# Gathers by step, resident down weights and another order of work in an attention and mixture-of-experts layer

## The chip, the cores and the metric

The kernel runs on one core of a Trainium2 chip. Its metric is the time of one execution on the device, in microseconds (us). A core has a matrix engine (TensorE, PE in the profile, with its weight loads as PEld), a vector engine (VectorE, DVE), a scalar engine (ScalarE, ACT), a general engine (GpSimd, POOL) that here also issues the indirect DMAs, and a sync engine (SyncE, SP) that issues nearly all other DMAs. Each engine works through its own queue of instructions in order. The engines wait for one another by semaphores.

## The reference

One transformer layer on four batches of 512 tokens with 256 features: attention with 16 heads and a linear position bias, a layer norm, a mixture of 64 experts of which each token takes 8, a shared expert, and a second layer norm.

```python
x = _layernorm(x + attention(x))              # 16 heads of 16, causal, ALiBi
logits = x @ gate_w.T                         # 2048 tokens x 64 experts
topv, topi = jax.lax.top_k(logits, 8)
rw = softmax(topv)                            # the weights of a token's 8 experts
W = zeros((N, E)).at[arange(N)[:, None], topi].set(rw)
gate, up = split(einsum('nh,eih->nei', x, gu_w))
inter_w = silu(gate) * up * W[:, :, None]
out = einsum('nei,ehi->nh', inter_w, dp_w)    # the down projection of each expert
out = out + sigmoid(x @ sh_gate1_w.T) * shared_expert(x)
x = _layernorm(x + out)
```

## The kernel before, in words

**Steps.** The experts are worked through in 16 steps of four experts (`QUAD`) for each of the four batches: 64 steps in all. This text calls them by batch and step, 0.0 to 3.15. A 128-token tile (there are four, t = 0 to 3, in a batch) has 30 places for an expert (`CELL`; 32 in the last four steps of batch 3), so that a step has 120 rows of tokens for each expert.

Four strands make a step. `gather` (letter g, L1020) brings the tokens to their places with matmuls against one-hot tiles (`px`), which ACT and DVE copy to `xt`; a pass serves four steps. `up` (u) first issues the load of the step's down weights `dq` on SP (L1038, 256 KB), then 32 matmuls `gu` (L1049), a tanh on ACT (L1057) and two products on DVE (L1058, L1059). `down` (d) multiplies with `dq` (L1081), copies the result `yq` with ACT (L1093) and writes it to DRAM, `rows_out`, from SP (L1094).

**The way back.** A token takes its eight results from `rows_out` by eight indirect gathers. `route` computes, for each token, the rows of its eight experts sorted from the largest (place k = 0) to the smallest (k = 7); as a step's rows are contiguous, a higher row is a later step. `fetch` (i) issues one gather per tile and place on POOL (L1160), 128 in all, into a ring of 8 buffers `got`; the slice of `rows_out` that the instruction names decides which writes it must wait for. `combine` (c) multiplies each gathered tile by its weight and adds it to `x` on DVE (L1171), and after a tile's last place comes the layer norm (L607 to L626) and the store. Gather n into the ring waits until combine n - 8 has read its buffer.

**The late steps.** The last four steps of batch 3 (3.12 to 3.15, `LATE`) aren't gathered: their results stay on chip (L1088, in the place of used weights), weights spread over the rows come from DRAM (`spread_in`, w, four DMAs on SP each), DVE masks them (`weigh`, e, L1120), and `collect` (k) multiplies and adds them (L1135, L1143). So the gathers of batch 3 need steps 3.0 to 3.11 alone. For batches 0 to 2, places 4 to 7 need steps up to 14 and places 0 to 3 all 16. In batch 3 every gather of before names the whole buffer, all twelve steps.

**What sets the order.** Nothing is left to a scheduler. Each strand is a Python generator; a string `ORDER` of one letter per turn (p projection, s scores, v context, o output, r routing, and those above) says which strand goes on next. So an instruction's place in its engine's queue is written out by hand, and each engine meets the strands in that order. A closing check (z) of three products `fine` and `fits` sets a flag; if it is set, a second, general program computes everything again.

**Memory.** `cxT` (two buffers), `scale` (two) and `avs` (two) belong to the attention and are idle once it is over. `dq` has four buffers.

Of the kernel before, what the change touches and what calls it, by code (L numbers as in the profile page):

```python
# [8 lines left out]
FP = mybir.dt.float32  # L9
# [3 lines left out]
ALU = mybir.AluOpType  # L13
AX = mybir.AxisListType

P = 128
HEADS, HD = 16, 16
# [9 lines left out]
ROOM = 32  # L27
GROUP = 16
# [9 lines left out]
    "pppppspppspsppsvvvsppvsvsvsvsvvspsovsvpsvvvspsppopposvvsvsoovsrrrvvsvspsvvvrhrosrrsvvsvrhrsvsrsrprhh"  # L38
    "rgvvvspogspprvphphporshvrvvsoorsprrgsvvvgsroghsvrgsrvvrvsrrsvsgvvsorvsrrgvvorsvsrosorsorrrrvvsvsvvvv"
    "tuguugguuggrhglogrgdrruuugrddrruuurrdorlgguuruuggdgrougrudgogrugllrugdudduggruuggrghrhhuuhgdhhdguuuu"  # L40
    "ghddgrrhugudguudrghgriiirgdgiguggruuuiiiuugicigcduigucigdcrgdigcuucgciuugddrczcccgigciiiiricduruuigg"
    "igugrgcguuiggcdgcihhucudhcuuhicddiughuuudcihggiiciugucddgirchhuiguuugdgcgccddggicciciuuucugcgguccgud"
    "guigciiicduccddccgcguugccggguiiguicchccuudugiiidcciigiiiiguucugigdgccuuigigchcidhiucduhhiuducghdchuu"
    "cgguudchcigghcuudigcuiugdgcidccdcigicuuiggcicuiguigiuccgudugggiiucicidcdccdcccruuccgggguuiciigcuwwug"
    "gccdugidgiiicichdgiuccugccggieguccugecuiiiicdiiduuuiucciccdcduiddwciicciiicicicuuiuuucciwccicciccccc"
    "uceecckdiiidkciicdciickicicicckicicckicicicicciiiiiiicickickiiccccccccccckcccz"
# [363 lines left out]
def kernel(  # L410
# [329 lines left out]
    def context():  # L740

        for b in range(B):
            cxT = cxs[b] = mpool.tile([P, KC, S], FP, tag="cxT", name=f"cxT_{b}", bufs=2)
            for c, par, n in units:
# [15 lines left out]
                avs = mpool.tile([P, S], FP, tag="avs", name=f"avs_{b}_{c}_{par}", bufs=2)  # L760
# [17 lines left out]
    def output():  # L778

        for b in range(B):  # L780
            scales = []
            for c in range(KC):
# [5 lines left out]
                scale = mpool.tile([P, S], FP, tag="scale", name=f"scale_{b}_{c}", bufs=2)  # L788
                for h in range(HEADS // KC):
                    nc.sync.dma_start(  # L790
                        out=scale[HD * h : HD * (h + 1), :],
                        in_=turned[b][part][h : h + 1, :].to_broadcast([HD, S]),
                    )
                scales.append(scale)
# [5 lines left out]
            for c in range(KC):  # L800
                nc.vector.tensor_tensor(cxT[:, c, :], cxT[:, c, :], scales[c], ALU.mult)
# [13 lines left out]
    codes, ats, w8s, shares = {}, {}, {}, {}  # L815

    def route():

        for b in range(B):
# [48 lines left out]
            nc.vector.tensor_tensor(row, row, chosen, ALU.mult)  # L868
            r8 = small.tile([P, NT, TOP], FP, tag="r8", name=f"r8_{b}")
# [6 lines left out]
            if not LATE[b]:  # L876
                part = slice(TOP // 2, TOP)
                nc.vector.tensor_scalar(at[:, :, part], near[:, :, part], SOON[b] - QUAD * SLOTS - 1.0, None, ALU.min)
# [28 lines left out]
            if LATE[b]:  # L907
# [6 lines left out]
                nc.vector.memset(rest[:, :, FIRST[b] :], 0.0)  # L914
# [9 lines left out]
                for t in range(NT):  # L924
                    nc.tensor.transpose(pt[: 2 * EL, t * P : (t + 1) * P], pair[:, t].rearrange("p w e -> p (w e)"), ident)
                flip = rpool.tile([P, TOP, NE], FP, tag="pick", name=f"flip_{b}", bufs=2)
# [106 lines left out]

    def up():

        for n, (b, q) in enumerate(steps):
            dq = late["pool"].tile([P, QUAD // 2, E], FP, tag="dq", name=f"dq_{b}_{q}", bufs=4)
            nc.sync.dma_start(out=dq, in_=dp[:, 2 * q : 2 * q + 2, :])  # L1038
# [86 lines left out]
    def collect():  # L1125

        for b in range(B):
# [13 lines left out]
            for t in range(NT):  # L1141
                part = xs[b][:, t, :]
                nc.vector.tensor_tensor(part, acc[t // 2][:, t % 2, 0:E], part, ALU.add)  # L1143
                yield
# [4 lines left out]
    for b in range(B):  # L1149
        if LATE[b]:  # L1150
            moves += [(b, t, k) for t in range(NT) for k in range(TOP)]
        else:
# [134 lines left out]
```

## Time and profile before

| | us |
|---|---|
| median of three runs | 483.08 (480.72 to 483.99) |
| the profiled execution | 479.91 |
| its span, first to last instruction | 477.4 |
| PE busy | 423.1 (89%) |
| DVE busy | 339.7 (71%) |
| ACT busy | 244.8 (51%) |
| POOL busy | 205.6 (43%) |

The profile is of one execution. A group's line gives: source line, engine, operation, result<-operands, shapes, count, then busy time and mean duration in ns, then the idle time of that engine just before, with what ended it. A row of the timeline starts with the start and the length in us; a bracket at its end is the idle time before it and its releaser. "DMA a<-b" in the chain is the wait for that transfer. The 40 slices of the page are 11.9 us each and hold tenths of busy time; PEclk is the clock that TensorE was granted.

### The profile page before, as it was taken

Reading aid. Unit: us, or ns where it says so; the run is one execution under the profiler, and the core shown is the slowest. Engines: PE = TensorE matmul, PEld = TensorE weight load, DVE = VectorE, ACT = ScalarE, POOL = GpSimd, SP = SyncE. Lnnn points to the kernel's source line nnn. Section 1 sums busy time; section 2 is a strip of 40 time slices with the busy share of each in tenths; the row PEclk is TensorE's granted clock in tenths of the full one; section 3 lists DMA queues with packets and bytes.
Section 4 is the critical chain, followed back from the end, with each engine's and each line's share of the span. In section 5 each row is a group of like instructions: output and inputs, shape, how many; then the busy total and the mean of one; then the engine's idle time right before and its main releaser. Section 6 shows DMA issues by size and latency. Waiting matters only on the chain.

```text
span 477.4 us, 12454 instructions
## 1 busy us (share of the span) xinstructions
PE 423.1 (89%) x4887; PEld 284.3 (60%) x4887; DVE 339.7 (71%) x922; ACT 244.8 (51%) x454; POOL 205.6 (43%) x238
## 2 busy tenths in 40 slices
PE   8999999998999989999999999999999997878100
PEld 3535454453644556876878778777787775765100
DVE  1522326798976888986786798889778898487474
ACT  2658647773578734446646547563566545322000
POOL 6424522253324610310027664266553666457771
PEclk9999999999999999999999999999999999897855
DMA  7900110000000043886868969889899899798342
GB/s 215 405 36 5 28 25 3 24 7 24 3 25 28 8 170 99 260 284 250 240 161 280 284 210 299 267 241 305 267 283 317 255 289 325 231 278 212 105 105 74
DMA packets 37238, 82.68 MB, mean 173 GB/s; under 512 B 8276, under 2 KB 14548, under 8 KB 36148
## 3 DMA queue, kind: packets, MB, share of 16 engines
q1 hardware_dynamic: 30484, 64.51, 43.1%
q0 software_dynamic: 6144, 16.79, 12.1%
q8 instruction: 40, 0.66, 0.6%
q10 hardware_dynamic: 544, 0.52, 0.3%
q14 instruction: 26, 0.21, 0.1%
HBM read 49.88 MB, written 31.92 MB: 171 GB/s over the span
## 4 chain that ended last, share of the span: by engine, by line
PE 68%; DVE 12%; DMA 8%; ACT 4%; issue 3%; POOL 2%; SPq 1%; DVEq 0%; POOLq 0%; ACTq 0%
PE gu L1049 19%; PE y L1081 11%; PE px L1020 9%; PE sT L724 8%; PE av L752 6%; DMA got<-rows_out,at 4%; PE pv L695 3%; PE pq L678 3%; PE pk L678 3%; PE po L808 2%; DMA dq<-in_dp_dram 2%; ACT yq L1093 2%; PE plT L828 2%; DVE x L1171 1%; PE sh L889 1%
## 5 line engine op out<-in xcount | busy, mean ns | idle before, releaser
L1160 POOL DMA_INDIRECT got<-rows_out,at x128 | 125.5, 980 | 128.8 <-DVE x L1171 57.8
L1049 PE MATMUL gu<-xt,gu_sb 128*64 128x120 f32 (+1 forms) x2048 | 118.9, 271 | 1.4 <-DVE ma L1059 1.4
L1049 PEld LDWEIGHTS gu<-xt,gu_sb 128*64 128x64 f32 x2048 | 106.2, 138 | 16.8 <-issue 14.1
L729 ACT ACTIVATE pr<-sT 128x768 f32<-128x768 f32 (+1 forms) x96 | 79.5, 884 | 29.4 <-PE sT L724 29.2
L734 POOL TENSOR_SCALAR_AFFINE_SELECT pr<-pr 128x512 f32<-128x512 f32 x64 | 41.8, 666 | 83.5 <-ACT pr L729 80.7
L1081 PE MATMUL y<-dq,ma 64*120 64x256 f32 (+1 forms) x512 | 68.5, 393 | 8.9 <-DMA dq<-in_dp_dram 5.6
L1093 ACT COPY yq<-y 120x1024 f32<-120x1024 f32 x60 | 59.9, 1012 | 29.4 <-PE y L1081 24.6
L1171 DVE SCALAR_TENSOR_TENSOR x<-got,w,x 128x256 f32<-128x256 f32 x128 | 62.7, 493 | 15.2 <-DMA got<-rows_out,at 13.5
L1081 PEld LDWEIGHTS y<-dq,ma 64*120 64x120 f32 (+1 forms) x512 | 44.5, 182 | 21.4 <-DVE x L1171 4.1
L1057 ACT ACTIVATE ma<-gu 128x240 f32<-128x240 f32 (+1 forms) x64 | 23.7, 371 | 59.9 <-PE gu L1049 51.5
L1010 ACT COPY xt<-px 128x192 f32<-128x192 f32 (+1 forms) x128 | 44.7, 365 | 17.0 <-PE px L1020 13.3
L724 PE MATMUL sT<-qT,kT 32*128 32x256 f32 (+3 forms) x512 | 51.9, 468 | 0.0
L1010 DVE COPY xt<-px 128x480 f32<-128x480 f32 x64 | 41.4, 650 | 14.2 <-ACT xt L1010 13.9
L942 POOL TENSOR_TENSOR pick<-pick,rest 128x512 f32<-128x512 f32 x16 | 21.3, 1334 | 48.2 <-ACT rest L903 25.3
L1020 PE MATMUL px<-hot,xh 64*128 64x288 bf16 x256 | 37.5, 287 | 4.8 <-ACT xt L1010 3.7
L752 PE MATMUL av<-pr,va 128*32 128x128 f32 (+3 forms) x512 | 40.2, 438 | 0.8 <-POOL pr L734 0.8
L1058 DVE SCALAR_TENSOR_TENSOR ma<-ma,gu 128x240 f32<-128x240 f32 (+1 forms) x64 | 25.6, 400 | 18.6 <-ACT ma L1057 18.4
L1020 PE MATMUL px<-hot,xl 64*128 64x288 bf16 x256 | 37.0, 283 | 0.0
L1020 PE MATMUL px<-hot,xm 64*128 64x288 bf16 x256 | 37.0, 282 | 0.0
L724 PEld LDWEIGHTS sT<-qT,kT 32*128 32x128 f32 x512 | 24.4, 183 | 19.7 <-issue 11.5
L752 PEld LDWEIGHTS av<-pr,va 128*32 128x32 f32 x512 | 13.8, 109 | 28.4 <-issue 17.6
L1059 DVE TENSOR_TENSOR ma<-gu,ma 128x240 f32<-128x240 f32 (+1 forms) x64 | 26.1, 408 | 2.2
(148 smaller groups left out, 488.6 us busy)
## 6 DMA issues: line engine op xcount, KB each, us to landing
rows_out<-yq SPq DMA_DIRECT2D x60, 480.0 KB, 5.2
dq<-in_dp_dram SPq DMA_DIRECT2D x64, 256.0 KB, 5.3
gu_sb<-in_gu_dram SPq DMA_DIRECT2D x8, 1024.0 KB, 11.1
scale<-turned SPq DMA_DIRECT2D x64, 32.0 KB, 1.8
got<-rows_out,at POOLq DMA_INDIRECT x128
gu_sb<-spread SPq DMA_DIRECT2D x16, 128.0 KB, 7.3
x<-in_x_dram SPq DMA_DIRECT2D x3, 512.0 KB
out_dram<-x SPq DMA_DIRECT2D x6, 256.0 KB
```

The costliest lines, as they stand in the source:

```text
L678: nc.tensor.matmul(ps, w_sb[n][:, kc, c * P : (c + 1) * P], xT[:, kc, :], start=(kc == 0), stop=(kc == KC - 1),)
L724: nc.tensor.matmul(s_ps[r // 2][:, r % 2, lo : lo + widths[m]], kTs[b][rows, c, kb * P : (kb + 1) * P], qTs[b][rows, c, par, kb * P :], st ...
L729: nc.scalar.activation(pr[:, 2 * i : 2 * i + 2, :], s_ps[i][:, :, : sum(widths)], AF.Exp, scale=1.0 / HD**0.5)
L734: nc.gpsimd.affine_select(out=pr[:, :, lo : lo + P], in_=pr[:, :, lo : lo + P], pattern=[[0, 4], [1, P]], compare_op=ALU.is_ge, fill=0.0, ...
L752: nc.tensor.matmul(av[32 * r : 32 * r + 32, kb * P :], vas[b % 2][:, kb, 8 * c + 2 * r + par, :], pr[:, r, lo : lo + w], start=(kb == 0), ...
L1010: copy(xt[:, kc, :, t * wide + lo : t * wide + hi], ps[:, kc, lo * GROUP : hi * GROUP].rearrange("p (s e) -> p e s", e=GROUP),)
L1020: nc.tensor.matmul(ps[:, kc, first : first + WIDTH * GROUP], parts[b][i][PART * half : PART * half + PART, t, kc * P : (kc + 1) * P], o[PA ...
L1049: nc.tensor.matmul(gu_ps[64 * e : 64 * e + 64, j, which, :], gu_sb[p // GUC][:, p % GUC, kc, which, 64 * e : 64 * e + 64], xt[:, kc, QUAD ...
L1081: nc.tensor.matmul(ys[:, e, j, :], a[64 * e : 64 * e + 64, j, :], dq[64 * e : 64 * e + 64, j, :], start=True, stop=True,)
L1093: nc.scalar.copy(yq.rearrange("s j e h -> s e j h"), ys)
L1160: nc.gpsimd.indirect_dma_start(out=g, out_offset=None, in_=rows_out[b][0 : SOON[b] - (QUAD * SLOTS if not LATE[b] and k >= HALF else 0)], ...
L1171: nc.vector.scalar_tensor_tensor(acc[:, t, :], got.pop(n), w8s[b][:, t, k : k + 1], acc[:, t, :], ALU.mult, ALU.add)
```

## The change

1. `BEFORE`: a gather for place k = 4, 5, 6, 7 names only the rows of the steps up to 1, 2, 3, 4 before the last (`reach`). This holds for batch 3 as well, counted from its twelve early steps. Routing clamps the row numbers place by place and multiplies a test of each into `fits`. The late steps' rows are cleared ahead of the sort in batch 3, so that its eight places count early rows alone.
2. Gathers and combines go by place: all four tiles of place 7, of 6, 5 and 4, then tile by tile places 0 to 3.
3. The down weights of steps 8 to 15 are loaded once, in batch 0, into buffers of the attention (two of `cxT`, one of `scale`, one of `avs`), and stay. 24 of 64 `dq` loads go. For this `scale` and `avs` become one buffer of two halves each.
4. `collect` adds two tiles at once (two instructions where there were four).
5. `ORDER` is another string.

```diff
+BEFORE = (0, 0, 0, 0, 1, 2, 3, 4)
...
+                if par == 0:
+                    both = mpool.tile([P, KC, S], FP, tag="avs", name=f"avs_{b}_{c}")
+                avs = both[:, par, :]
...
+    def reach(b, k):
+        return SOON[b] - BEFORE[k] * QUAD * SLOTS
...
+            if LATE[b]:
+                nc.vector.memset(row[:, :, FIRST[b] :], 0.0)
...
-            if not LATE[b]:
-                part = slice(TOP // 2, TOP)
-                nc.vector.tensor_scalar(at[:, :, part], near[:, :, part], SOON[b] - QUAD * SLOTS - 1.0, None, ALU.min)
+            for k in range(TOP):
+                if BEFORE[k]:
+                    end = reach(b, k) - 1.0
+                    nc.vector.tensor_scalar(at[:, :, k], near[:, :, k], end, None, ALU.min)
+                if BEFORE[k] > 1:
+                    nc.vector.scalar_tensor_tensor(
+                        fits[:, 0:NT], near[:, :, k], end + 0.5, fits[:, 0:NT], ALU.is_le, ALU.mult
+                    )
...
+    def stay(n):
+        bed, place = divmod(n, 2)
+        if bed not in beds:
+            tag, bufs = (("cxT", 2), ("cxT", 2), ("scale", 1), ("avs", 1))[bed]
+            old = mpool.tile([P, KC, S], FP, tag=tag, name=f"bed{bed}", bufs=bufs)
+            beds[bed] = old.rearrange("p k s -> p (k s)").rearrange("p (i w e) -> p i w e", i=2, w=QUAD // 2)
+        return beds[bed][:, place]
...
-            dq = late["pool"].tile([P, QUAD // 2, E], FP, tag="dq", name=f"dq_{b}_{q}", bufs=4)
-            nc.sync.dma_start(out=dq, in_=dp[:, 2 * q : 2 * q + 2, :])
+            if q < NQ // 2:
+                dq = late["pool"].tile([P, QUAD // 2, E], FP, tag="dq", name=f"dq_{b}_{q}", bufs=4)
+            elif b == 0:
+                stays[q] = dq = stay(q - NQ // 2)
+            else:
+                dq = stays[q]
+            if q < NQ // 2 or b == 0:
+                nc.sync.dma_start(out=dq, in_=dp[:, 2 * q : 2 * q + 2, :])
...
     for b in range(B):
-        if LATE[b]:
-            moves += [(b, t, k) for t in range(NT) for k in range(TOP)]
-        else:
-            moves += [(b, t, k) for t in range(NT) for k in range(HALF, TOP)]
-            moves += [(b, t, k) for t in range(NT) for k in range(HALF)]
+        moves += [(b, t, k) for k in range(TOP - 1, HALF - 1, -1) for t in range(NT)]
+        moves += [(b, t, k) for t in range(NT) for k in range(HALF)]
...
-                out=g, out_offset=None, in_=rows_out[b][0 : SOON[b] - (QUAD * SLOTS if not LATE[b] and k >= HALF else 0)],
+                out=g, out_offset=None, in_=rows_out[b][0 : reach(b, k)],
```

The last two lines of the two order strings show the fifth point; i and c are gathers and combines, u, d and k the matmuls of up, down and collect:

```
before: "gccdugidgiiicichdgiuccugccggieguccugecuiiiicdiiduuuiucciccdcduiddwciicciiicicicuuiuuucciwccicciccccc"
        "uceecckdiiidkciicdciickicicicckicicckicicicicciiiiiiicickickiiccccccccccckcccz"
after:  "dgicucgcuwuiigcchgcuucuuiigccgduuiiggcdgddcicicgiiiuucccccicgcugidwuiicgccudigiccccgcdciiuuueicicucc"
        "ucidiiuwwuuiiiiudciciecudidekccidikckiciciezcicickicicickicicickicccckccccccccccz"
```

## The prediction

> **What bounds the kernel now.** I read the page first, then the chain that ended last, then the timeline of PE and POOL in the last 80 us, then busy time by stage.
>
> ```profile
> span 477.4 us, 12454 instructions
> PE 423.1 (89%) x4887; PEld 284.3 (60%) x4887; DVE 339.7 (71%) x922; ACT 244.8 (51%) x454; POOL 205.6 (43%) x238
> ...
> PE   8999999998999989999999999999999997878100
> ...
> POOL 6424522253324610310027664266553666457771
> PEclk9999999999999999999999999999999999897855
> ```
>
> PE is full for 33 slices and gone in the last three. So there are two parts: a long one that PE sets, and a tail that something else sets. What is it? The timeline of POOL and DVE from 426 us on:
>
> ```profile
> 426.54 0.94 POOL L1160 DMA_INDIRECT got<-rows_out,at  x1 [3.48 <-DMA gu_sb<-spread]
> 427.79 1.07 POOL L1160 DMA_INDIRECT got<-rows_out,at  x1 [0.30 <-DVE x L1171]
> ...
> 465.98 1.07 POOL L1160 DMA_INDIRECT got<-rows_out,at  x1 [0.30 <-DVE x L1171]
> ...
> 469.05 0.48 DVE L1171 SCALAR_TENSOR_TENSOR x<-got,w,x 128x256 f32<-128x256 f32 x1 [0.27 <-DMA got<-rows_out,at]
> ...
> 472.44 0.41 DVE L626 TENSOR_SCALAR x<-x,mv,rstd 128x256 f32<-128x256 f32 x1
> ```
>
> From 426.54 to 467.05 POOL issues 32 gathers back to back, one in 40.51/32 = 1.27 us: all of batch 3. Nothing else waits for long there; this is the tail. From the last gather's end to the span's end are 10.35 us: landing, a combine, a late add, the last norm and the store. The first gather waited for rows: the named releaser is the transfer beside them, but the instruction names the whole buffer, and the last rows in it are those of step 3.11. That step's down matmul is here, in PE's timeline:
>
> ```profile
> 402.71 1.03 PE L1081 MATMUL y<-dq,ma 64*120 64x256 f32 x8
> 407.42 1.61 PE L1081 MATMUL y<-dq,ma 64*120 64x256 f32 x8 [3.67 <-DMA dq<-in_dp_dram]
> 408.95 4.64 PE L1049 MATMUL gu<-xt,gu_sb 128*64 128x120 f32 x64
> ...
> 417.34 1.13 PE L1081 MATMUL y<-dq,ma 64*120 64x256 f32 x8
> ```
>
> 3.11 starts at 417.34; its rows can be gathered 9.2 us later (copy, write, landing), and the end comes 60.1 us after it. The reader also sees the one large PE stall: 3.8 waits 3.67 us for its `dq`, and runs slowly afterwards, 1.61 against 1.03, and 4.64 for two ups against 3.50 at 182.65 us. By stage (PE, PEld, DVE, ACT, POOL busy, clock, DMA share, GB/s):
>
> ```profile
> 360.00:400.00 40.00, 38.26 (x548) 29.76 (x544) 34.02 (x97) 22.05 (x45) 21.00 (x22) 1.00 0.93 279
> 400.00:417.30 17.30, 13.62 (x176) 11.25 (x172) 10.76 (x25) 6.15 (x10) 8.84 (x10) 0.90 0.85 289
> sum 248.60, PE 237.31 PEld 185.67 DVE 201.57 ACT 132.72 POOL 100.96; mean PE 33.90 PEld 26.52 DVE 28.80 ACT 18.96 POOL 14.42
> ```
>
> The sum is over 168.7 to 417.3 us, where the experts are worked through: PE 95%, DVE 81%. Before 400 us PE is idle for 11.97 us in all, then 3.67.
>
> **The change part by part.** The same PE work stands ahead of 3.11 in both listings of the instructions, and the same behind it (three ups, four downs, the four groups of collect). So I ask when 3.11 starts, and how long the end is behind it.
>
> *Down weights.* 24 loads of 256 KB leave SP and the DMA engines, 6.3 of 82.7 MB. Worth on the path: the stall of 3.67 and the slow stretch after it, (1.61 - 1.03) + (4.64 - 3.50) = 1.72. 3.11 would start at 417.34 - 5.39 = 411.95. The other loads were hidden behind PE work; steps 0 to 7 stay as they were, 5 to 7 us of PE work ahead of their use, against 5.3 us to landing. New is that the load of 0.10 takes the buffer of `cxT` right after the last matmul that reads it and stands 5.7 us of PE work ahead of its use: between 0 and the 3.67 of the stall above, I take +1, as it is nearest to the loads that just fit. The halves of `avs` and `scale` fall free a unit later, ten us of attention: 0, bound by the 1.5 us of PE's largest stall there.
>
> *The tail.* Place 7 now needs rows up to 3.7, 6 up to 3.8, 5 up to 3.9, 4 up to 3.10, and 16 gathers of places 0 to 3 need 3.11. If POOL were free, 16 x 1.27 = 20.3 us would follow the rows: last gather 9.2 + 20.3 = 29.5 us after 3.11 starts. But POOL is not free. PE work from 3.8 to 3.11 is about 9.5 us (ups 1.86, downs 1.03, gather halves 0.4), so 3.8's rows come about when 3.11 starts, and 28 gathers then take 35.5 us, with a little waiting between: last gather 29.5 to 33 us after 3.11. Behind it, norms now overlap: the twelfth of the 16 ends 5.1 us before the last, lands in 2.5, add 0.7, norm of three tiles 4.57 (459.69 to 464.26), four combines 2.0, last norm 2.86, store 4.55: 12.1 us behind the last gather. The end is thus 41.6 to 45 us behind the start of 3.11; I take 44, for 60.1 before: -16. PE's own rest takes 26 us now (417.34 to 443.57) and is done by then.
>
> *DVE.* This is the bill. The new order puts 18 more combines (0.49 each), two more norms (4.0 each, 429.21 to 433.24) and the new clamps ahead of 3.11: per batch four at 0.27 and three at 0.16, less one of 0.30 in three batches, 5.3 us. 8.9 + 8.0 + 5.3 = 22 us, less a masking of 0.75, to the 201.57 in 243 us: 92%. If they fit into DVE's gaps they cost nothing, as combines did up to now; if the gaps are all needed, 21 us. Where it is tight is the stretch from 2.15 to 3.11: counted by letter, DVE goes from some 41 to 51 us there (41 combines, 2.5 norms, 13 ups at 0.81, 12 copies at 0.65), against 46.5 us of PE. So at least 4.5; I take 6.
>
> *Combines that wait.* DVE is in order: a combine that waits for rows holds the products behind it, which PE's downs need. From a step's down to its gather took 9.2 us from its start at 3.11, and a gather's data takes 2 to 3 more, some 12 us. Before, the first combine stood 12.8 us of PE work or more behind the step it needs, outside the tail. Now 8.1 us for place 7 of batch 0, 10.8 for 6 and 7 of batch 2, and 9.4, 6.8 and 5.5 in batch 3 (where DVE's lag, counted above, covers the wait). 0 to 4 us each; I take +2.5, for the first.
>
> POOL's 0.3 us between gathers and `collect` (two adds of 0.7 for four of 0.42) stay where they are. Sum: 411.95 + 1 + 6 + 2.5 = 421.5 for 3.11, + 44 = 465.5 for the span, + 2.51 (479.91 - 477.4) = **468**. The profiled execution is 0.7% under the median of the runs; the change is -12, 2.5%.
>
> A rule of the Trainium skill speaks against the change. The gathers' mean is 980 ns, with 940 the least and 1345 the most, beside a DVE that is 85% busy from 360 to 400 us.
>
> ```profile
> L1160 POOL DMA_INDIRECT got<-rows_out,at x128 | 125.5, 980 | 128.8 <-DVE x L1171 57.8
> ...
> L1171 DVE SCALAR_TENSOR_TENSOR x<-got,w,x 128x256 f32<-128x256 f32 x128 | 62.7, 493 | 15.2 <-DMA got<-rows_out,at 13.5
> ```
>
> By "SBUF — State Buffer", section "Who interferes with whom", DVE and GpSimd hold a shared pair of ports exclusively, and the one that comes second waits for the whole instruction. By that, gathers beside a fuller DVE would stretch; the trace shows it at 4% over the least, so it is a rival only.
>
> **The rivals.**
> *PE alone* (15%). DVE fits into its gaps, no combine waits: 3.11 at 412, + 41.6 to 44, + 2.5 = 456 to 458.5. For it: DVE is idle for 47 us in this stretch now. Against: the last 50 us are full.
> *DVE takes the bound* (13%). All 21 us become path, 3.11 at 434, + 44 + 2.5 = 480.5: no change. For it: 92% on an engine that both waits for PE and is waited for.
> *Combines block the queue* (11%), the slower side. If the early combines hold DVE and through it PE, with rows and gathers as late as behind 3.11 in the trace (gather at 426.54, its combine at 433.44: 16 us from the down), the shortfalls are 8 (batch 0), 5 (batch 2) and 6.6, then some 3 each for the next two in batch 3, which stack: 25 us, and DVE's 6: 3.11 at 443, end 490. It decides from about 4 us over the 12 that I take.
> *Ports* (3%). Each of the 28 gathers at 1345 instead of 980: +10, 478.
> *No finer waits, or the guard* (3%). If a gather still waited for all rows, the tail keeps 60: 484. But the listing shows a different DMA semaphore for places 6, 5, 4 and 0. The second program would cost hundreds of us; worked through for these inputs, no token's row passes a bound.
>
> **How the numbers follow.** Forecast 55% (461 to 475), rivals 15, 13, 11, 3, 3. The likeliest gives 468. Leaving out the slow end of the rivals and half of the fast one's, 454 to 482 holds 8 in 10. One per cent, about what a measurement here tells from no change, is 478.2 to 487.9. Faster: 55 + 15 + 3 + a part of the DVE case, 0.76; the same: the rest of that case and the unchanged tail, 0.13; slower 0.11.
>
> **What would show it.** Right: no `dq` wait behind batch 0; 3.11's down near 421; POOL gathering without a gap from about then, 21 or so gathers behind it instead of 32; the end 42 to 45 us behind 3.11; DVE over 88% in the expert stage. Wrong: PE waiting for `ma` products by more than 10 us in all, DVE waiting for `got` by more than 10 us ahead of 3.11, or POOL idle for rows in the tail.

## The result, and the profile after

The changed kernel takes 477.73 us (median; 474.31 to 483.01), the kernel before on the same chip 481.62: a ratio of 0.9906 (0.9881 to 0.9931). Run once more beside other kernels it gave 0.9948 (0.9908 to 0.9987). So the gain is 0.5 to 0.9%, under the one per cent that the prediction gives as what a measurement tells from no change; 2.5% was forecast. The profiled execution took 478.21 us, with a span of 476.5, 0.9 less than before. The page of the changed kernel, parts 1 and 2:

```profile
span 476.5 us, 12378 instructions
PE 427.4 (90%) x4887; PEld 287.3 (60%) x4887; DVE 337.5 (71%) x946; ACT 244.2 (51%) x454; POOL 204.5 (43%) x238
...
PE   8999999989999999999989999899899989976900
...
POOL 6433522255513610220145556255661677364770
PEclk9999999999999999999989999999999999898965
```

PE is now at work one slice longer, with a hole (7 and 6) just ahead, and POOL's row, full in the last slices before, has holes too (the 3 and the 4 near its end). PE's timeline where step 3.5, step 3.6 with 3.7, and step 3.11 go down:

```profile
405.76 1.13 PE L1115 MATMUL y<-dq,ma 64*120 64x256 f32 x8 [1.80 <-DMA dq<-in_dp_dram]
407.33 3.67 PE L1115 MATMUL y<-dq,ma 64*120 64x256 f32 x16
...
431.78 2.07 PE L1115 MATMUL y<-bed,ma 64*120 64x256 f32 x8 [3.66 <-DVE marks L1151]
```

3.8's wait for weights is gone, as forecast; 3.5 waits instead, and 3.11 for its products (`marks` is only the instruction right behind them). And 3.11 starts at 431.78, where 421.5 was forecast and 417.34 was measured before. The end comes 44.7 us behind it (forecast 44, before 60.1). These rows of POOL's timeline are the starts that stand behind a gap of over 0.5 us, and the last gather:

```profile
409.60 0.94 POOL L1191 DMA_INDIRECT got<-rows_out,at  x1 [0.87 <-DVE x L1202]
...
416.97 0.94 POOL L1191 DMA_INDIRECT got<-rows_out,at  x1 [6.43 <-DVE x L1202]
...
423.58 0.94 POOL L1191 DMA_INDIRECT got<-rows_out,at  x1 [1.84 <-DVE rstd L625]
...
433.65 0.94 POOL L1191 DMA_INDIRECT got<-rows_out,at  x1 [5.37 <-DVE x L1202]
...
463.29 0.95 POOL L1191 DMA_INDIRECT got<-rows_out,at  x1 [0.30 <-DVE st L609]
```

416.97 is batch 3's first gather (place 7), 433.65 the first of place 5, which needs the rows of 3.9. Before, all 32 gathers ran without a gap; now they lose 6.9 us: from first start to last 46.3 us, where 31 spacings of 1.27 are 39.4. The gaps at 416.97, 423.58 and 433.65 are not the ring's, as the combines that free these buffers had ended by 415.50, 417.46 and 425.35; they are waits for the rows of 3.7, 3.8 and 3.9.

What holds up 3.5's weights and 3.9's rows stands in SP's queue (start, length with issue time, number):

```profile
394.53 3.59 SPq L1141 DMA_DIRECT2D gu_sb<-spread  x4
398.16 2.18 SPq L1072 DMA_DIRECT2D dq<-in_dp_dram  x3
...
417.91 0.32 SPq L1128 DMA_DIRECT2D rows_out<-yq  x1
418.32 3.03 SPq L1141 DMA_DIRECT2D gu_sb<-spread  x4
421.57 1.08 SPq L1128 DMA_DIRECT2D rows_out<-yq  x1
```

The new order puts the loads of the late steps' spread weights (w, four of 128 KB a step) ahead of the loads for 3.5 to 3.7, and between the rows of 3.8 and 3.9. In the kernel before, the first eight of them stood together, ahead of the weights of 3.7 and of the steps behind it:

```profile
387.12 7.07 SPq L1107 DMA_DIRECT2D gu_sb<-spread  x8
394.24 0.43 SPq L1038 DMA_DIRECT2D dq<-in_dp_dram  x1
...
398.10 2.29 SPq L1038 DMA_DIRECT2D dq<-in_dp_dram  x3
```

In the changed kernel the three `dq` loads go out at 398.16, and 3.5's down starts 7.6 us later. 3.9's write is issued by 422.65, and the gather that names it starts 11.0 us later; 3.7's rows took 4.5 (issued by 412.44, gather at 416.97). In the second execution the same gather at 432.86 names the write itself:

```profile
432.86 0.94 POOL L1191 DMA_INDIRECT got<-rows_out,at  x1 [6.43 <-DMA rows_out<-yq]
```

And DVE's timeline shows what 3.11 waits for: two place-7 combines, ahead of its products, wait for gathers. These gathers started at 419.55 and 420.80, so that their data took 8.6 and 9.6 us, where the prediction counted 2 to 3.

```profile
428.16 0.48 DVE L1202 SCALAR_TENSOR_TENSOR x<-got,w,x 128x256 f32<-128x256 f32 x1 [1.84 <-DMA got<-rows_out,at]
430.40 0.48 DVE L1202 SCALAR_TENSOR_TENSOR x<-got,w,x 128x256 f32<-128x256 f32 x1 [1.75 <-DMA got<-rows_out,at]
430.80 0.40 DVE L1092 SCALAR_TENSOR_TENSOR ma<-ma,gu 128x240 f32<-128x240 f32 x1
```

Is DVE full, as feared? By stage (columns as before; the second row ends at 3.11), no: 208.0 us in 263.0, 79%. Up to 3.11 it carries 6.4 us more than before (201.57), not 22.

```profile
168.70:400.00 231.30, 219.57 (x3002) 169.75 (x2996) 185.53 (x517) 121.63 (x262) 97.08 (x99) 0.99 0.74 228
400.00:431.70 31.70, 23.90 (x310) 19.23 (x306) 22.47 (x72) 12.94 (x25) 15.38 (x16) 0.94 0.89 229
sum 263.00, PE 243.46 PEld 188.98 DVE 208.00 ACT 134.57 POOL 112.46; mean PE 121.73 PEld 94.49 DVE 104.00 ACT 67.29 POOL 56.23
```

### The profile page after: what moved, and what is told of

It reads as the page before. It is cut to its first block, busy times and chain, and to the rows that moved or that the text cites. A ratio compares the mean times of both kernels' runs of the same rounds, so it can differ in the third digit from the quotient of the medians.

```text
span 476.5 us, 12378 instructions
## 1 busy us (share of the span) xinstructions
PE 427.4 (90%) x4887; PEld 287.3 (60%) x4887; DVE 337.5 (71%) x946; ACT 244.2 (51%) x454; POOL 204.5 (43%) x238
## 2 busy tenths in 40 slices
DMA packets 33782, 76.39 MB, mean 160 GB/s; under 512 B 7892, under 2 KB 14164, under 8 KB 32692
## 5 line engine op out<-in xcount | busy, mean ns | idle before, releaser
L1127 ACT COPY yq<-y 120x1024 f32<-120x1024 f32 x60 | 60.0, 1012 | 37.1 <-PE y L1115 31.9
L1202 DVE SCALAR_TENSOR_TENSOR x<-got,w,x 128x256 f32<-128x256 f32 x128 | 59.4, 482 | 18.0 <-DMA got<-rows_out,at 16.9
L1026 DVE COPY xt<-px 128x480 f32<-128x480 f32 x64 | 41.5, 651 | 23.3 <-ACT xt L1026 23.2
L1091 ACT ACTIVATE ma<-gu 128x240 f32<-128x240 f32 (+1 forms) x64 | 23.8, 371 | 59.8 <-PE gu L1083 58.8
L1115 PE MATMUL y<-bed,ma 64*120 64x256 f32 (+1 forms) x256 | 35.9, 406 | 4.4 <-DVE marks L1151 3.7
L1115 PE MATMUL y<-dq,ma 64*120 64x256 f32 x256 | 35.8, 404 | 4.4 <-DMA dq<-in_dp_dram 3.4
L958 POOL TENSOR_TENSOR pick<-pick,rest 128x512 f32<-128x512 f32 x12 | 16.4, 1362 | 39.6 <-ACT rest L918 28.3
L1115 PEld LDWEIGHTS y<-dq,ma 64*120 64x120 f32 x256 | 23.4, 187 | 10.7 <-issue 4.5
```

Source lines behind the costliest of these rows:

```text
L1026: copy(xt[:, kc, :, t * wide + lo : t * wide + hi], ps[:, kc, lo * GROUP : hi * GROUP].rearrange("p (s e) -> p e s", e=GROUP),)
L1115: nc.tensor.matmul(ys[:, e, j, :], a[64 * e : 64 * e + 64, j, :], dq[64 * e : 64 * e + 64, j, :], start=True, stop=True,)
L1127: nc.scalar.copy(yq.rearrange("s j e h -> s e j h"), ys)
L1202: nc.vector.scalar_tensor_tensor(acc[:, t, :], got.pop(n), w8s[b][:, t, k : k + 1], acc[:, t, :], ALU.mult, ALU.add)
```

## The experiments

**Theories.** 1: the new order makes queues stall ahead of 3.11 (combines for gathers, loads of weights behind spread loads), and gives back what the tail gains. 2: the features cost it themselves (resident weights, clamps, one buffer for two halves, finer waits). 3: DVE is full. Two refinements came up later: 1a, the spread loads are what delays; 1c, the end hangs on the rows of 3.7 and 3.9 and on POOL, not on 3.11.

In the diffs of the order, a turn is written as strand and step: c0.07 is the combine of batch 0, tile 0, place 7; dq is the first turn of an up, the one that issues the load, where there is one (for steps 8 to 15 of batches 1 to 3 there is none), U and D the matmuls of up and down, and G those of gather. Ratios are to the kernel before on the same chip. Chips differ: the first four kernels (old order, three moves, third move alone, no resident weights) met one on which the kernel before takes 525.5 us, here called the slow chip; there ACT alone waits up to 42.6 us at its tanh (L1091) for releases that the records don't name, so that expectations in us can't be read there, and the changed kernel itself was not run on it.

**The features in the old order** (twice).

```diff
-ORDER = <the changed kernel's>
+ORDER = <the string before, less its last two k>
```

> The changed kernel with the order of work of the kernel before (two collect letters fewer, since the late add has two steps less): the resident weights, the finer waits, the clamps and the new sequence of rows stay, only the units stand as they did before. Theory 1 (the new order is what delays step 3.11): 3.11's down starts near 412 us (417.34 less the 5.39 of the stall that the resident weights take away), POOL comes to batch 3 as soon as it has done batch 2, some 5 us sooner than before, and gathers on without a gap: last gather near 458, end near 470, time near 471 to 473, faster than the changed kernel by 1% or more. Theory 2 (resident weights, clamps, one buffer for two halves, finer waits cost PE time themselves): 3.11 starts at 425 us or later in this order too, time 480 or more. Theory 3 (DVE's sheer load): the same work stands ahead of 3.11 on DVE as before, less than in the changed kernel, so this theory too gives 412 to 415; it differs from theory 1 in the runs that move single units.

> The changed kernel with the order of work of the kernel before, once more, beside the changed kernel itself. Theory 1 (the new order delays step 3.11 by stalls, and gives back what the tail gains): faster than the changed kernel by 0 to 1.5%; on a chip that takes some 481 us for the kernel before, 3.11's down starts near 412 us, no combine waits ahead of 3.11, the end comes 58 us behind it or a little less, time 471 to 474. Theory 2 (the resident weights, clamps and finer waits themselves cost): slower than the changed kernel, 3.11 at 425 us or later.

Measured: 519.95 us on the slow chip, 0.9859 (0.9803 to 0.9915); 477.11 on the other, 0.9925 (0.9897 to 0.9953), beside 0.9948 for the changed kernel. 3.11 starts at 415.17, the span is 474.3; both are 3 to 4 us later than theory 1 expected. Against the trace before, each step is 1.2 us later after attention, 3.4 later from 1.6 on and 2.2 earlier from 3.9 on: 3.8's stall was worth 5.6. So theory 2 falls, as far as it says that the features delay 3.11 to 425 or later, and 18.6 us of 3.11's start (433.78 in the changed kernel beside it) come with the order. But an early 3.11 buys little here either. POOL's timeline shows why:

```profile
400.11 0.95 POOL L1191 DMA_INDIRECT got<-rows_out,at  x1 [2.76 <-DVE x L1202]
...
461.50 0.95 POOL L1191 DMA_INDIRECT got<-rows_out,at  x1 [0.30 <-DVE rstd L618]
```

From 400.11 to 462.45 it issues 48 gathers with no gap over 0.8 us: the last 16 of batch 2, then batch 3. The finer waits do work (first gather at 421.68, before 426.54), until POOL's backlog and the ring are the bound: the combine that frees the buffer of that first gather ends at 421.41.

**Three moves in the new order** (twice), and two of them.

```diff
 ... r54 [+c0.07 c0.17 c0.27 c0.37]     # all_three, c0_u: from 6 to 13 turns ahead
 ... dq3.7 [+w0 w1]                     # all_three: from ahead of dq3.5 and of dq3.10
 ... c3.17 [+G3.3.3b D3.10 dq3.11 U3.11 dq3.12] c3.27 c3.37     # all_three, u_first, c0_u
```

> The changed kernel with three moves in its order. (a) The first four combines of batch 0 stand behind the read of step 1.0's tile passes instead of ahead, 3 us later. (b) The spread weights of late steps 3.12 and 3.13 are loaded right behind the load of step 3.7's down weights, not ahead of the loads for 3.5 to 3.7 and not between the rows of 3.8 and 3.9. (c) Step 3.11's up, and with it its products, stand ahead of the place-7 combines of tiles 2 and 3 of batch 3. Amount of work on every engine unchanged. Theory 1 (queues: something that waits stands ahead of something that PE needs): each move takes away a stall of 1.8 to 3.7 us and the 3.4 us of half clock behind it, 3 to 5 us each, 3.11 starts near 421 us, the time is 467 to 470. Theory 3 (DVE is simply full): the stalls move elsewhere, 3.11 stays within 3 us of 431.8, the time within 3 us of the changed kernel.

> The changed kernel with move (c) alone: step 3.11's up and its products stand ahead of the combines of place 7, tiles 2 and 3, of batch 3. Those two wait 1.84 and 1.75 us for their gathers, then 3.11's down waits 3.66 us for its products and 3.4 us run at half clock. Theory 1: the wait is taken away, 3.11 starts 3 to 5 us sooner, near 427 to 429 us, and the time falls by 2 to 4 us. Rival (the tail is set by the rows that come late through the busy DMA queues, and by POOL behind them, not by 3.11): 3.11 starts sooner, but the first gather that needs 3.8's rows starts where it did, the end stays within 1 us.

> The three moves (combines of batch 0 later, spread weights of 3.12 and 3.13 earlier, up of 3.11 ahead of two combines), once more, beside the changed kernel. Theory 1: each takes away a stall and the half clock behind it; on a chip of some 481 us 3.11 starts near 421, time 467 to 470; on a slow chip 1% or more under the changed kernel. Theory 3 (DVE full, stalls only move): within 3 us of the changed kernel.

> The changed kernel with two of the three moves: batch 0's first four combines 3 us later, and 3.11's up with its products ahead of two combines of batch 3; the spread weights stay. Theory 1 with the tail tied to 3.11: 3.11 starts near 426 instead of 433, the end 44 us behind it, time 471 to 473. Theory 1c (what counts is when the rows of 3.7 and of 3.9 are in memory, since POOL waits for just these, 6.4 and 6.1 us, and gathers without a gap behind them): 3.11 starts 5 us or more sooner, but 3.7's and 3.9's rows only 2 us sooner (batch 0's stall), so the last gather and the end come 1 to 3 us sooner, time 476 to 478, and the end is 47 us or more behind 3.11.

Measured: on the slow chip 0.9970 (0.9932 to 1.0009) for all three and 1.0030 (0.9980 to 1.0081) for the third alone, nothing to tell apart. On the others all three gave 479.05 us, 0.9950 (0.9915 to 0.9985), the first and third 477.53, 0.9916 (0.9888 to 0.9945). The traces say more. Batch 0's move brings 1.9 to 2.1 us in both. The spread loads' move only moves the stall: eight of them in one go stand ahead of the rows of 3.4, the write lands late, ACT has no free `yq`, and PE stops 4.59 us at 413.86.

```profile
412.57 1.01 ACT L1127 COPY yq<-y 120x1024 f32<-120x1024 f32 x1 [5.32 <-DMA rows_out<-yq]
```

In the kernel with the first and third move, 3.11 starts at 426.95 instead of 433.78, without a wait of its own. (The two executions of the changed kernel differ here by 2.0 us, 433.78 and 431.78.) But its span is 476.1, against 477.6 and 476.5: the end is 49.1 us behind 3.11. POOL's gaps there:

```profile
415.74 0.94 POOL L1191 DMA_INDIRECT got<-rows_out,at  x1 [6.82 <-DVE x L1202]
429.31 0.94 POOL L1191 DMA_INDIRECT got<-rows_out,at  x1 [3.85 <-DVE x L1202]
437.88 1.00 POOL L1191 DMA_INDIRECT got<-rows_out,at  x1 [3.74 <-DMA rows_out<-yq]
```

So 1c holds: 4.8 to 6.8 us sooner at 3.11 were 0.4 to 1.5 at the end, as POOL still waits for the rows of 3.7, 3.9 and 3.10.

**The old order up to 3.8, the new one behind it.**

```diff
-ORDER = <the changed kernel's>
+ORDER = <what stands up to D3.8 in it, in the sequence of the order before> + <the rest>
```

> The changed kernel's features; the order of the kernel before up to the down of step 3.8, and behind it what was left in the changed kernel's order. Theory 1: up to 3.8 there are no stalls that the kernel before did not have, less the wait for 3.8's weights: 3.8 starts near 403 us on a chip of some 481; behind it the new order's stalls ahead of 3.11 (5.7 us in the changed kernel's trace) stay, so 3.11 near 418; the end 45 us behind, time 464 to 468: the fastest of the four. If the tail needs the work that the new order did earlier (norms and combines of batch 2), 3.11 starts early but the end comes 50 us or more behind it, time 470 or more. Theory 2: no faster than the changed kernel.

Measured: 482.41 us, 1.0027 (0.9994 to 1.0061). 3.8 starts early (406.7 for its copy), and then PE waits 15.02 us for the products of 3.10, which stand in DVE's queue behind batch 2's combines and norms, and these behind POOL's backlog. The expectation missed that the two orders fill POOL differently.

```profile
426.68 2.07 PE L1115 MATMUL y<-bed,ma 64*120 64x256 f32 x8 [15.02 <-DVE ve L617]
```

**No spread loads**, in the changed kernel and in the kernel before.

```diff
-            for t in range(NT):
+            for t in range(0):
                 nc.sync.dma_start(out=wide[ROOM * t : ROOM * (t + 1)], in_=spread[b]...)
```

> The changed kernel without the sixteen loads that spread the expert weights of the four late steps (3.12 to 3.15) over the partitions; the weights collected there are then whatever lies in the buffer, so the late steps' part of the result is left out of the comparison of what is computed. Theory 1a (these loads, 128 KB each in pieces of 512 bytes, delay what stands beside them on SP's queue and in the DMA engines: the weights of 3.7, the rows of 3.9): the wait of 3.7 (1.9 us and half clock behind it) and POOL's gap for the rows of 3.9 (6.1 us) go, the combines of place 7 wait less; 3.11 starts at 424 to 427 instead of 432 to 434, last gather near 457, time 469 to 473, 6 us or more under the changed kernel. Rival 1b (the combines that wait for gathers in DVE's queue, whatever the DMA engines do): 3.11 within 3 us of the changed kernel's, time within 3 us.

> The kernel before without the same sixteen loads (late steps' part left out as there). Theory 1a with the new order more exposed to them: here the wait of 3.8's weights (3.67 us, 1.7 of slow matmuls) goes, and POOL's 3.5 us ahead of batch 3: 5 us or less off 482. If they cost the kernel before as much as the changed one (6 us or more in both), they are no reason for the gain that is missing.

Measured: 470.65 us, 0.9789 (0.9753 to 0.9825), and 478.01, 0.9914 (0.9886 to 0.9942). So the loads cost the changed kernel some 7 us and the kernel before some 4: 1a holds, and only the difference, about 3, is the new order's own loss by them. In the kernel before, 3.8's wait for its weights falls from 3.67 to 0.70 us: the stall that the prediction credits to the resident weights is in good part made by the spread loads ahead of them. Its profiled execution (480.17 us, the longest of eleven) shows nothing of the 4 us: it loses 2.7 us at 277 us (see the last section), and its first gather of batch 3 starts at 427.39, 11.0 us behind 3.11. So the 4 us rest on the medians alone.

(Where the expectations speak of 3.7's weights, it is 3.5's down that waits; its load and those of 3.6 and 3.7 go out together.) 3.11 starts at 425.64, and POOL's gap at 433 is gone. The two place-7 gathers have their data 6 us after their starts, not 8.6 and 9.6. The same stretch of time of the changed kernel and of the one without the loads, by busy time, clock, DMA share, GB/s:

```profile
422.00:428.00 6.00, 5.04 (x78) 4.14 (x74) 3.93 (x17) 1.78 (x3) 3.50 (x4) 1.00 0.95 119
```

```profile
422.00:428.00 6.00, 4.06 (x60) 3.51 (x62) 3.56 (x10) 1.40 (x2) 4.48 (x6) 1.00 0.98 207
```

The DMA engines are as busy in both, but move 119 GB/s with the spread loads and 207 without. The packets in the first trace show what delays the rows of 3.9: their write, issued by 422.65, has no packet before 427.64, while the 256 packets of the four spread loads run from 420.68 to 428.48. The write stands behind these loads. Without them, it is issued by 417.40 and its first packet starts at 418.39. In the stretch shown a packet of a gather takes 0.75 us (0.52 without the loads), and one of a spread load 0.19, where the shortest take 0.08.

Piece size, which the expectation blames, isn't it: without the 16 loads the page counts 1280 packets less (33782 to 32502) and 2.1 MB, 80 a load; the 24 `dq` loads have 144 each. In both cases 16 of them are under 512 bytes, and the others carry 2 KB each. Why packets take longer here stays open.

**Combines of batch 2 sooner, in the old order.**

```diff
 ORDER of old_order, with each combine from late in batch 1 to the middle of batch 3 up to four places sooner in the combines' own sequence,
 and each gather as soon as the ring has a free buffer
```

> The changed kernel's features in the order of the kernel before, with the combines from batch 1's last to batch 3's first ones four places sooner in their own sequence, and gathers issued as soon as the ring of eight buffers has one free. In the old order with these features POOL gathers without a gap from 400.1 to 462.5, 48 gathers, and waited for a free buffer 22.8 us of the time behind 360; data lies 8 to 12 us in the ring before its combine. Theory 4 (in the old order POOL's backlog sets the end, not 3.11): POOL gets 4 to 6 us ahead, first gather of batch 3 at 416 to 418 instead of 421.7, last at 457 to 459, time 470 to 473, 4 us or more under the old order's 477. Rival: the combines ahead of the products hold DVE and through it PE; 3.11 starts 3 us or more later than 415, the time stays at 476 to 480.

Measured: 477.20 us, 0.9919 (0.9890 to 0.9947), against 0.9925 without: nothing. POOL did get ahead (first gather of batch 3 at 418.85), and waits ahead of the first gathers of place 7 and of place 5 instead:

```profile
418.85 1.07 POOL L1191 DMA_INDIRECT got<-rows_out,at  x1 [3.24 <-DVE x L1202]
...
431.45 0.95 POOL L1191 DMA_INDIRECT got<-rows_out,at  x1 [2.45 <-DVE x L1202]
```

These are not waits for rows. The writes of 3.7 and 3.9 had been issued by 408.50 and 413.84, and each gather starts 0.3 us behind the end of the combine that frees its ring buffer (418.59 and 431.18). That combine stands in DVE's queue behind a layer norm and, in the first case, a step's products; the data of the first had landed at 408.4. So the next bound behind the backlog is the ring again, through DVE's order.

**The spread loads behind 3.11.** All work is done; w0 and w1 stand where w2 and w3 are.

```diff
-... U3.4 [w0] dq3.5 ...  D3.8 [w1] dq3.10 ...
+... D3.11 [w0 w1] ... e0, e1 later          # w_late; w_late_c0_u: with the first and third move too
+... [e0] c3.24 [e1 k0] c3.34 [k1] c3.00 [e2] c3.01 [e3 k2] ...   # late_products: e three to six combines later
+... dq3.12 [U3.12] c3.27                     # late_products_u
```

> The changed kernel with the spread loads of late steps 3.12 and 3.13 moved from ahead of 3.5's and 3.9's work to right behind the down of 3.11, and the products of the first two with them a little later; all work is done. If place is what costs (theory 1a): 3.7's weights and 3.9's rows come as in the run without the loads, 3.11 starts at 424 to 428, last gather near 457 to 460, time 471 to 474, 1 to 1.5% under the changed kernel's 478. If the bytes cost wherever they lie (the gathers of the tail land later beside them, collect ends later and the last adds wait): 476 to 479, with DVE waiting for gathers or for acc in the tail.

> The same with the two other moves (batch 0's first four combines 3 us later; 3.11's up ahead of two combines of batch 3). Theory 1: the 2 us of batch 0 come on top, 3.11 starts at 419 to 423, time 468 to 472, the best of all. Theory 1c: 3.11's own start is worth nothing, only the 2 us of batch 0 are: 1 to 2 us under w_late.

> As the run with all moves and the spread loads behind 3.11's rows, and the four products with the spread weights three to six combines later in DVE's queue, collect behind them; all work is done. If the 4.5 us that POOL stops in the tail are due to combines that stand behind these products: they fall below 1.5, the last gather ends near 456 instead of 459.3, time 470 to 472, 3 us under 474.2. If collect then comes too late for the last adds: DVE waits for acc at the end and the time stays at 474.

> The same, and 3.12's up with its products right behind 3.11's. PE's wait of 3.1 us at 428 us (3.12's successor waits for a PSUM that 3.12's products hold) goes. PE's own rest ends some 10 us ahead of the last gather, so this is off the path: within 1 us of late_products. If the place-7 combines that it pushes back by 1 us hold POOL's ring: 1 us slower.

Measured: 477.24 us, 0.9899 (0.9860 to 0.9939); with the two moves 474.22, 0.9820 (0.9785 to 0.9854); with the products later 471.77, **0.9800** (0.9766 to 0.9834); with 3.12's up sooner 472.62, 0.9813 (0.9776 to 0.9851). The first two are 3 and 2 us above what theories 1a and 1 expected of them, and 477.24 lies where the rival put it (the bytes cost wherever they lie); the third shows that place and order of the products make up the difference. In the first, 3.5's wait and the gap for 3.9's rows are gone and 3.11 starts at 426.63; but the tail stops anew. In the second, where this is plainer, DVE's products with the spread weights wait for their loads, combines stand behind them, and POOL stands at its full ring:

```profile
443.02 0.75 DVE L1154 SCALAR_TENSOR_TENSOR gu_sb<-gu_sb,marks 128x512 f32<-128x512 f32 x1 [2.84 <-DMA gu_sb<-spread]
```

```profile
444.44 0.95 POOL L1191 DMA_INDIRECT got<-rows_out,at  x1 [4.85 <-DVE x L1202]
```

With these products a few combines later that gap goes, and POOL's largest ones behind the first gather are these (the second without a releaser that the profile shows):

```profile
428.27 0.98 POOL L1191 DMA_INDIRECT got<-rows_out,at  x1 [1.24 <-DMA rows_out<-yq]
...
436.83 0.95 POOL L1191 DMA_INDIRECT got<-rows_out,at  x1 [2.16 <-issue]
```

This is the fastest of all, ahead of the kernel before by 2.0% and of the changed kernel by 1 to 1.5. PE's waits around 3.12 were off the path, as expected: 3.0 us of them in the last kernel instead of 4.6 changed nothing.

**The same move in the old order.**

```diff
 ORDER of old_pull4, with
-... U3.6 [w0 w1] dq3.7 ...
+... D3.12 [w0 w1] w2 ... [e0 e1] e2
```

> The changed kernel's features in the old order with combines of batch 2 four places sooner, and the first two steps' spread loads behind 3.11's rows as well. In the run without this move POOL waited 2.9 us for the rows of 3.7 and 2.1 for those of 3.9. If the loads' place is what delays these rows: both waits shrink, 3 to 5 us sooner, time 472 to 474. If it is PE's time for 3.7 (its copy at 407.1, gather at 418.9): no change, 476 to 478.

Measured: 484.51 us, 1.0038 (1.0007 to 1.0069), a miss: worse. The expectation reads the two waits as waits for rows, and the trace of the run before it shows the ring. Both are there again, 3.25 and 2.45 us, and each ends 0.3 us behind its combine. So this run decides nothing on the rows. On top of that, the products with the spread weights wait so long that `collect` is 13.49 us late, and POOL stops 6.92 us in the tail, for a ring buffer too.

```profile
441.56 2.04 PE L1169 MATMUL acc<-gu_sb,gu_sb 32*128 32x256 f32 x13 [13.49 <-DVE gu_sb L1154]
```

**No resident weights in the new order** (twice).

```diff
-            if q < NQ // 2:
+            if True:
                 dq = late["pool"].tile([P, QUAD // 2, E], FP, tag="dq", name=f"dq_{b}_{q}", bufs=4)
...
-            if q < NQ // 2 or b == 0:
+            if True:
                 nc.sync.dma_start(out=dq, in_=dp[:, 2 * q : 2 * q + 2, :])
```

> The changed kernel without resident weights: every step loads its down weights into the four ring buffers as the kernel before did; order, waits and clamps as changed. If the resident weights are worth what the stall of 3.8 in the kernel before cost (3.67 us and 1.72 of slow matmuls behind it): 5 us or more slower than the changed kernel, some 483 us, with waits of downs for their weights at 3.8 to 3.11, and more, up to 490, if the loads land as late as the gathers beside the spread weights do (9 to 11 us). If they are worth nothing (loads hidden, or the buffers of avs, scale and cxT cost attention as much): within 2 us of the changed kernel, with the attention of batch 0 to 1 shorter by as much as it now is longer.

> The changed kernel without resident weights, on a chip of these runs. The prediction put the resident weights at 5.4 us (the stall of 3.8 and what follows it). With the order of the changed kernel each load of down weights stands behind spread loads in SP's queue twice more, so 5 to 12 us slower than the changed kernel, 483 to 490, with waits for weights at 3.5 to 3.11; if the loads are hidden in the new order: within 2 us of 478.

Measured: 535.98 us on the slow chip, 1.0200 (1.0161 to 1.0240), and 498.33, 1.0335 (1.0285 to 1.0385). For the second, against the changed kernel's 0.9906 and 0.9948 on other chips, that is some 4%, 19 us, well over the 12 allowed. PE's waits for weights, in this second execution and in the changed kernel (us in total, times, longest), make up 17.6 of them:

```profile
PE y L1115 <- DMA dq<-in_dp_dram: 21.0, 9, 7.9
```

```profile
PE y L1115 <- DMA dq<-in_dp_dram: 3.4, 3, 1.8
```

## Why the prediction was wrong

The two numbers of its sum first. The tail, 44 us, was measured at 44.7; the start of 3.11, 421.5, was 431.8. So the sum failed in the second; but the tail's working failed too, and its number held by luck, because 3.11 was late together with what the end hangs on. It also has a slip of its own: 28 gathers that start when 3.11 does end 35.5 us behind it, not 29.5 to 33, which with the 12.1 gives 47.6, not 44. In the two kernels of the table whose new order lets 3.11 start without a wait (two moves; spread loads late) the end is 49.1 and 47.3 us behind it. What the runs put in its place: the end is the first gather of batch 3, plus 40.4 us for 32 gathers (before: 426.54 to 467.05 is 40.5), plus POOL's gaps, plus some 12 (11.8 to 12.4 in the table; 10.4 before; forecast 12.1).

| kernel | 3.8 starts | 3.11 starts | first gather of batch 3 | gaps | last gather ends | span |
|---|---|---|---|---|---|---|
| before | 407.4 | 417.3 | 426.5 | 0 | 467.1 | 477.4 |
| changed | 415.7 | 431.8 | 417.0 | 6.9 | 464.2 | 476.5 |
| features, old order | 407.0 | 415.2 | 421.7 | 0.4 | 462.5 | 474.3 |
| two moves | 413.0 | 427.0 | 415.7 | 7.7 | 463.8 | 476.1 |
| no spread loads | 410.7 | 425.6 | 414.0 | 2.6 | 456.9 | 468.9 |
| spread loads late, two moves, products later | 409.2 | 422.1 | 412.2 | 4.4 | 457.0 | 469.4 |

(Gaps: first to last start less 31 spacings of 1.27.) The forecast's own last gather would have ended at 421.5 + 31.9 = 453.4. The measured 464.2 is 10.8 later: some 3.7 because 3.8 starts at 415.7 and not 9.5 ahead of 421.5, and 6.9 by the gaps.

*"The other loads were hidden."* This is the step that failed. It looked at the loads that the change removes and at the one of 0.10, and left out the 16 spread loads, which the new order moves past others in SP's queue. They make 3.5 wait 1.80 us (and 1.6 at half clock behind it: 3.67 for two downs of 1.03), and hold up the rows of 3.9 by 6.5 (11.0 us from issue to gather, for 4.5). The prediction put them at nothing; leaving them out of the changed kernel brings 7 us, and its span to 468.9, 3.4 over the forecast 465.5 instead of 11.0. Some 4 of the 7 the kernel before pays too. The worth of the resident weights was right for the old order alone (5.39 forecast, 5.6 measured there); in the new order they save some 19.

*POOL "with a little waiting between"*: 6.9 us of gaps, 5.1 of it ahead of place 5 for the rows of 3.9, by the above, and 1.5 ahead of place 6 for those of 3.8.

*Combines that wait, 2.5.* Right in place and size for batch 0: the first combine waits 2.54 us, PE 1.99, and moving four combines gave 1.9 to 2.1. For batch 3, "DVE's lag covers the wait" was wrong: the two combines cost 3.11 some 3 to 5 us (4.8 to 6.8 sooner with both moves, 1.9 of it batch 0's), because their data took 8.6 and 9.6 us and not 2 to 3. With both moves no more than 1.5 reached the end.

*DVE, +6.* Wrong: 6.4 us of work came, not 22, at 79%; 13 more combines start ahead of 3.11, not 18, and the items that the prediction lists for the tight stretch add up to 48.4 us, not 51. The two moves, which take no work from DVE, start 3.11 4.8 to 6.8 us sooner; theory 3 falls with the term.

*+1 for the load of 0.10, 0 for the halves of `avs` and `scale`.* No down of batch 0 waits for weights. But the first down starts 2.4 us later than before (183.7 for 181.3), and 1.2 later with the features in the old order; 0.4 of that is within what two executions differ. Some 3 us more go in batches 1 and 2, where DVE's waits for ACT at `xt` rose from 13.9 us in all to 23.2. Neither was tried by itself: what causes these four or five us stays open.

Of the prediction's signs of being wrong one came, POOL idle for rows in the tail; of its signs of being right only the end's distance from 3.11, by luck as said.

*The rivals.* "DVE takes the bound" gave a time near the measured one, 480.5, by a mechanism that isn't there. "Combines block the queue" had the mechanism: six waits, 7.5 us ahead of 3.11. Its price was too high, 25, and it counted them at 3.11, where the end no longer hangs. The ports rival is out: the gathers' mean is 976 ns (before 980), beside the same DVE. "No finer waits" is out by the first gather's start.

## What to carry to other kernels

When an order of work is rewritten, list for each queue every transfer that changes its neighbours, not those alone that the change adds or removes; here 16 loads that nobody edited cost the changed kernel 7 us, some 3 more than the kernel before, where the whole edit gained 4. A time measured behind some event (the end 44 us behind 3.11) predicts only if the end hangs on that event: follow the resource that runs without a gap, here POOL's 32 gathers, and ask what each gap in it waits for. And a combine, product or load that waits belongs behind everything in its queue that could go on without it.

## What the runs showed of the hardware

**The clock is granted in stretches of 3.41 us, and a stall's price depends on where it falls.** In all traces half speed comes in multiples of that length on one grid. The same stall of batch 0 (PE waits for `x1T`) takes 2.38 us in the kernel with late spread loads and 2.31 in the one without them. By stretches of that grid (PE busy first, clock third from the end), of the first and of the second:

```profile
238.44:241.85 3.41, 1.05 (x4) 0.17 (x2) 1.68 (x4) 0.40 (x1) 2.53 (x3) 1.00 0.54 177
241.86:245.27 3.41, 3.40 (x10) 1.43 (x10) 1.71 (x4) 0.58 (x1) 2.37 (x3) 0.50 0.34 102
```

```profile
237.62:241.03 3.41, 1.82 (x12) 0.50 (x9) 0.99 (x3) 0.73 (x2) 2.65 (x3) 1.00 0.70 228
241.04:244.45 3.41, 2.71 (x18) 1.39 (x20) 2.54 (x7) 1.07 (x2) 2.66 (x3) 1.00 0.36 101
```

In the first the whole stall lies in one stretch (2.36 idle of 3.41), and the next one runs at half speed; two `plT` matmuls take 1.97 us instead of 1.07. In the second it is cut by the boundary (1.6 idle in the first part), and nothing follows. The copy of step 1.0 differs by 1.7 us from this (257.2 against 255.5). Over the sixteen traces of the other chips, up to 440 us, a stretch at full speed with less than 1.7 us idle was always followed by full speed, one with 1.85 or more by half, with one exception (1.99), and between these both came. On the slow chip half speed also came behind 1.2 to 1.6 us. The Trainium skill ("TensorE: Matmul & The Clock Gate", Part 1) has a free-running window of about 3.4 us, which agrees, and half speed after at least one idle window; here half a window was enough. A step of the order can thus gain or lose some 2 us by the moment of a stall, as in this pair. The kernel before without spread loads lost 2.7 us at 277 us in a pause of 2.09 with half speed behind it, where the kernel before paused 0.77 at full speed.

**Chips differ, and not by a factor.** On the one that is 9% slower the kernel before took 525.5 us; the features in the old order had about the same ratio there (0.986 and 0.9925), but the new order without resident weights was 2.0% (1.6 to 2.4) behind the kernel before there, and 3.4% (2.9 to 3.9) elsewhere, by six runs each. Why is not shown.
